# A vision-transformer layer on one core: PSUM slots of scores and mixes, and SBUF slots of the exps, taken strictly in turn

## The chip, the core and the metric

The kernel runs on one core of a Trainium2 chip. A core has five engines with instruction queues of their own: TensorE (PE), VectorE (DVE), ScalarE (ACT), GpSimd (POOL) and SyncE (SP, which here only issues transfers). They wait for each other through semaphores. The metric is the device time of one execution in microseconds; of the kernel before, six runs are at hand.

## The reference

The input is 16 images of 3x512x512. Each is cut into 1024 patches of 16x16, which become tokens of 256 values. One transformer layer follows. What matters here is its attention, eight heads of 32, in which the keys pass through a Fourier series of 256 frequencies before they are used:

```
q, k, v = to_heads(q), to_heads(k), to_heads(v)
k = kan_transform(k, kan_a, kan_b)      # sum over f of a_f*sin(f*k) + b_f*cos(f*k)
dots = einsum('bhqd,bhkd->bhqk', q, k) * scale
attn = softmax(dots, axis=-1)
out = einsum('bhqk,bhkd->bhqd', attn, v)
```

After that come the output projection, a second layernorm, a shared three-layer network, and four expert networks of which each token uses the two with the highest gates.

## The kernel before, in words

**Pairs and groups.** An image has four pairs of heads, and a pair two blocks of 512 queries, so there are 128 attention blocks. A block goes through the 1024 keys in eight chunks `kc` of 128. The Fourier series of an image's keys is worked off in 32 groups, 512 in all.

**A group** (lines 945 to 1083). Angles come from DRAM as whole numbers, spread over the partitions, into two "wave" tiles `w` (eight slots) and one `f`. POOL multiplies them by each partition's frequency (L1009), ACT takes the sines (L1019), TensorE mixes the two wave tiles into one PSUM tile `kan` of 128x1024 (L1039), DVE multiplies that by `f` (L1053), and TensorE adds up over partitions (L1072). `kan` is free when the product on DVE is done.

**A chunk of a block** (lines 1132 to 1199). TensorE computes the scores of a chunk into one PSUM tile `sT` of 128x1024 (L1137). ACT takes the exp (L1154). For an even chunk it writes it to an SBUF tile `es`, and the score's PSUM tile is free. For an odd chunk it writes it in place, into PSUM, and DVE then adds the even chunk's exp and writes the sum to an SBUF tile `both` (L1169); only then is the odd chunk's PSUM tile free. (The values `v` are stored so that the even chunk's exp and the pair's sum give the right weighted sum.) TensorE weighs the values with `es` or `both` (L1184), into one accumulator `av`. `es` and `both` are free when their weighing is done, `es` also needs the pair sum done.

**Slots.** `kan` and `sT`, 512 + 1024 = 1536 tiles, come from one PSUM pool `big` of two slots under one tag (lines 126, 1034, 1135). A tile fills two banks, so the slots are banks 0 and 1, and 2 and 3. `es` and `both`, 1024 tiles, come from the SBUF pool `esp` of five slots under one tag (lines 121, 1153, 1168). With one tag the framework picks the slot that a new tile takes. In the built program the slot taken from `big` is in 1485 of 1534 cases the one whose last reader was written down first; whoever writes to it waits for that reader.

**What sets the order.** All instructions are laid by a planner in the kernel itself. TensorE's order is a string written out by hand, `ORDER` (line 65): M is a mix, S a score, W a weighing, R an adding-up, and digits are steps of four chains that carry tokens, norms, projections and the feed-forward networks. Eleven of the sixteen images share one repeated piece of it. The other engines are filled in greedily by due times that the planner reckons with costs of its own (`others`, line 408). Where it lays a score or a mix it holds that the tile two before must be free (L443), and for an exp or a pair sum that the tile five before must be free (L1159). Each engine works through its queue in that order and stops at the first instruction whose semaphores are not there.

```
at = begin(PE, deps + (bigs[-2:-1] if user else []))   # L443: the tile two before
old = att * NT + kc - NES                               # L1160: the tile five before
```

Of the kernel before, what the change touches and what calls it, by code (L numbers as in the profile page):

```python
# [11 lines left out]
FP = mybir.dt.float32  # L12
# [3 lines left out]
PSUM = bass.MemoryType.PSUM  # L16
DRAM = bass.MemoryType.DRAM

P = 128
# [3 lines left out]
N = 1024  # L23
NT = N // P
# [24 lines left out]
NES = 5  # L49
# [41 lines left out]
def plain_path(ctx: ExitStack, tc: tile.TileContext, a: dict, out: bass.AP, verdict: bass.AP):  # L91
# [14 lines left out]
    def pool(name, bufs, space=None):  # L106
        kw = {} if space is None else {"space": space}
        return ctx.enter_context(tc.tile_pool(name=name, bufs=bufs, **kw))
# [9 lines left out]
    wp = pool("wp", NW)  # L118
    fp = pool("fp", GS)
    srcp = pool("srcp", 1)  # L120
    esp = pool("esp", NES)
    q4p = pool("q4p", 2)
    ffp = pool("ffp", 1)
    ff2 = pool("ff2", 2)
    smp = pool("smp", 1)
    big = pool("big", 2, PSUM)
    side = pool("side", 1, PSUM)
    redp = pool("redp", 1, PSUM)
    avp = pool("avp", 1, PSUM)
# [131 lines left out]
    def put(engine, queue, cost, deps, key, action):  # L261

        queues[engine].setdefault(queue, []).append((cost, deps, key, action))
# [29 lines left out]
    def side_tile(name):  # L293

        i = chains[now["chain"]]["bank"] = banks(now["chain"])[0][1]
        return side.tile([P, 512], FP, tag=f"side{i}", name=name)
# [729 lines left out]
    kan = {}  # L1026
    red = {}
    bigs = []

    def mix(g):  # L1030


        def action():
            ps = kan[g] = big.tile([P, N], FP, tag="big", name="kan")
            for j in range(2):
                w = w_tiles.pop((g, j))
                for blk in range(2):
                    for r in range(2):
                        nc.tensor.matmul(  # L1039
                            out=ps[ds(64 * j + 32 * blk, 32), ts(r, 512)],  # L1040
                            lhsT=coef[ts(r, 64)].rearrange("p e f j -> p (e f j)"),
                            rhs=w[ts(r, 64), ts(blk, 512)],
                            start=True,
                            stop=True,
                        )

        deps = [("sine", g, 0), ("sine late", g)]
        put(PE, "M", 0.86, deps, ("mix", g), action)
# [79 lines left out]
    scores = {}  # L1128
    exps = {}
    acc = {}  # L1130

    def score(att, kc):
        def action():
            q4 = bands_of_queries[att]
            ps = scores[kc] = big.tile([P, 1024], FP, tag="big", name="sT")
            for s in range(2):
                nc.tensor.matmul(  # L1137
                    out=ps[:, ts(s, 512)],
                    lhsT=k4[:, 2 * s + kc // 4, ts(kc % 4, P)],
                    rhs=q4[:, s, :],  # L1140
                    start=True,
                    stop=True,
                )

        deps = [("stacked", att // 2), ("q4", att)]
        put(PE, "S", 0.47, deps, ("score", att, kc), action)

    def exponential(att, kc):
        def action():
            now["table"] = AF.Exp  # L1150
            ps = es = scores[kc]
            if kc % 2 == 0:
                es = exps[kc] = esp.tile([P, 1024], FP, tag="es", name="es")
            nc.scalar.activation(es, ps, AF.Exp, scale=SCALE)  # L1154

        deps = [("score", att, kc)] + (tile_free(att, kc) if kc % 2 == 0 else [])
        put(ACT, "fixed", 0.99, deps, ("exp", att, kc), action)

    def tile_free(att, kc):  # L1159
        old = att * NT + kc - NES  # L1160
        if old < 0:
            return []
        deps = [("av", *divmod(old, NT))]
        return deps if old % 2 else [*deps, ("sum", *divmod(old + 1, NT))]

    def pair_sum(att, kc):
        def action():
            both = exps[kc] = esp.tile([P, 1024], FP, tag="es", name="both")
            nc.vector.tensor_add(both, scores[kc], exps[kc - 1])  # L1169

        deps = [("exp", att, kc - 1), ("exp", att, kc)] + tile_free(att, kc)
        put(DVE, "sum", 1.16, deps, ("sum", att, kc), action)
# [114 lines left out]
    for rd in range(B * RI + 2):  # L1287
        groups = range(GS * rd, min(GS * rd + GS, total))
        att = rd - 2
# [26 lines left out]
    ps = side_tile("okT")  # L1316
# [583 lines left out]
def vit_layer(tc: tile.TileContext, a: dict, out: bass.AP):  # L1900
    with tc.tile_pool(name="verdict", bufs=1) as vp:
        verdict = vp.tile([1, 1], mybir.dt.int32, tag="verdict", name="verdict")
        plain_path(tc, a, out, verdict)
        bad = tc.nc.values_load(verdict[0:1, 0:1], min_val=0, max_val=1)
        with tc.If(bad > 0):
            general_path(
                tc, *(ap for name, ap in a.items() if name not in PLAIN_ONLY), out
            )
# [149 lines left out]
```

## Time and profile before

| | |
|---|---|
| Median of six runs | 3968.06 us (3959.48 to 3974.56) |
| The profiled execution | 3971.46 us, span 3969.9 us |
| Mean granted TensorE clock | 0.984 |
| TensorE busy | 3726.7 us, 94% of the span |
| ScalarE busy | 3259.3 us, 82% |
| GpSimd busy | 3191.6 us, 80% |
| VectorE busy | 3116.9 us, 79% |
| Transfers | 915.93 MB, 231 GB/s on average |

The profile is one execution on the chip. Busy time says how long an engine worked, and the list of waits says what ended the idle time of an engine: "PE sT L1137 <- ACT es L1154: 51.0, 71, 3.2" means that TensorE stood idle before score matmuls until an exp had ended, 51.0 us in all, 71 times, 3.2 us at most. PEld is TensorE's loading of weights, which runs ahead of the matmuls and carries their waits; a wait there costs only what its matmul also waits. "Issue" is idle time for which no other instruction is found. A line of the order in time gives start, duration, engine, line, operation, tiles, and in brackets the idle time before it.

### The profile page before, as it was taken

What the parts mean: (1) busy time and instruction counts of PE and PEld (TensorE: products, weight loads), DVE (VectorE), ACT (ScalarE), POOL (GpSimd) and SP (SyncE); (2) the same over time, 40 slices, a digit from 0 to 9 for tenths busy, and PEclk for the clock granted to TensorE, in tenths of its full rate; (3) what the DMA queues carried; (4) which work ended last, traced back from release to release, by engine and by line L of the source; (5) the groups of instructions that cost most, each with busy time, mean ns of one, the idle gap of its engine ahead of it and who ended that gap; (6) DMA issues with size and microseconds to landing.
All of it is one profiled execution on the core that took longest, in us unless ns stands there. A gap on an engine that the chain in (4) does not pass through costs nothing. (4 is left out here: it accounts for less than half of the span.)

```text
span 3969.9 us, 93620 instructions
## 1 busy us (share of the span) xinstructions
PE 3726.7 (94%) x35701; PEld 1808.4 (46%) x35701; DVE 3116.9 (79%) x4715; ACT 3259.3 (82%) x3875; POOL 3191.6 (80%) x2312
## 2 busy tenths in 40 slices
PE   6888999999999999999999999999999999999988
PEld 4324344454444445454454444545444454534434
DVE  4777878878787888878878787887878878788873
ACT  2687888888888888888888888888888888888983
POOL 4988888788888878888888888878878888888860
PEclk9999999999999999999999999999999999999999
DMA  7887877888888788878888788888878888778750
GB/s 233 267 234 207 265 220 232 250 234 258 215 251 239 218 262 235 250 225 246 240 244 250 216 241 241 224 252 237 242 222 250 243 235 252 212 233 246 217 165 21
DMA packets 587580, 915.93 MB, mean 231 GB/s; under 512 B 58828, under 2 KB 177524, under 8 KB 587124
## 3 DMA queue, kind: packets, MB, share of 16 engines
q1 hardware_dynamic: 580880, 906.98, 78.4%
q8 instruction: 285, 4.67, 0.5%
q10 hardware_dynamic: 6244, 2.88, 0.3%
q14 instruction: 171, 1.40, 0.1%
HBM read 758.64 MB, written 150.99 MB: 229 GB/s over the span
## 5 line engine op out<-in xcount | busy, mean ns | idle before, releaser
L1009 POOL TENSOR_TENSOR w<-w,lane 128x1024 int32<-128x1024 int32 x1024 | 1924.7, 1895 | 388.7 <-DMA w<-ud 288.6
L1019 ACT ACTIVATE w<-w 128x1024 f32<-128x1024 int32 x1024 | 1011.6, 1047 | 52.4 <-POOL w L1009 48.7
L1009 POOL TENSOR_TENSOR f<-f,lane 128x1024 int32<-128x1024 int32 x512 | 970.1, 1895 | 103.6 <-DVE f L994 99.5
L1137 PE MATMUL sT<-q,k 128*128 128x512 f32 x2048 | 746.8, 464 | 163.7 <-DVE both L1169 55.2
L1169 DVE TENSOR_TENSOR both<-sT,es 128x1024 f32<-128x1024 f32 x512 | 624.3, 1219 | 308.7 <-ACT sT L1154 295.5
L1154 ACT ACTIVATE sT<-sT 128x1024 f32<-128x1024 f32 x512 | 517.4, 1011 | 266.9 <-PE sT L1137 197.4
L1053 DVE TENSOR_TENSOR f<-kan,f 128x1024 f32<-128x1024 f32 x512 | 609.1, 1214 | 144.8 <-ACT f L1019 91.3
L994 DVE STREAM_SHUFFLE f<-src 128x1024 int32<-128x1024 int32 x512 | 687.9, 1360 | 0.4
L1154 ACT ACTIVATE es<-sT 128x1024 f32<-128x1024 f32 x512 | 521.4, 1018 | 123.8 <-PE sT L1137 112.8
L1137 PEld LDWEIGHTS sT<-q,k 128*128 128x128 f32 x2048 | 344.8, 192 | 557.5 <-ACT es L1154 172.8
L1039 PE MATMUL kan<-w,coef 64*32 64x512 f32 x8192 | 556.4, 604 | 21.3 <-ACT w L1019 19.9
L1019 ACT ACTIVATE f<-f 128x1024 f32<-128x1024 int32 x512 | 517.3, 1047 | 0.0
L1184 PE MATMUL av<-both,v 128*32 128x256 f32 x4096 | 326.9, 390 | 4.1 <-DVE both L1169 3.8
L1184 PE MATMUL av<-es,v 128*32 128x256 f32 x4096 | 323.1, 386 | 3.6 <-DVE rc L1225 3.4
L1184 PE MATMUL av<-both,ones 128*32 128x256 f32 x4096 | 321.9, 385 | 0.0
L1072 PE MATMUL red<-f,pack 128*32 128x512 f32 x2048 | 301.8, 614 | 4.4 <-DVE f L1053 2.5
L1208 DVE RECIPROCAL rc<-av 128x256 f32<-128x256 f32 x128 | 224.4, 1753 | 66.1 <-PE av L1184 66.0
L1039 PEld LDWEIGHTS kan<-w,coef 64*32 64x32 f32 x8192 | 119.5, 106 | 303.4 <-issue 131.2
L301 PE MATMUL tok<-wt,x 128*128 128x256 f32 x960 | 226.4, 387 | 16.3 <-DMA w1s<-in_sW 13.1
L301 PEld LDWEIGHTS tok<-wt,x 128*128 128x128 f32 x960 | 181.3, 192 | 73.0 <-issue 20.4
L1184 PEld LDWEIGHTS av<-es,v 128*32 128x32 f32 x4096 | 110.5, 109 | 195.8 <-issue 153.7
L1184 PEld LDWEIGHTS av<-both,v 128*32 128x32 f32 x4096 | 115.0, 110 | 170.3 <-issue 95.6
(154 smaller groups left out, 4823.1 us busy)
## 6 DMA issues: line engine op xcount, KB each, us to landing
w<-ud SPq DMA_DIRECT2D x2048, 256.0 KB
q<-qd SPq DMA_DIRECT2D x512, 128.0 KB
k<-kd SPq DMA_DIRECT2D x128, 512.0 KB
x<-in_xT SPq DMA_DIRECT2D x128, 384.0 KB
ud<-u SPq DMA_DIRECT2D x64, 512.0 KB
ud<-ui SPq DMA_DIRECT2D x64, 512.0 KB
src<-ud SPq DMA_DIRECT2D x512, 64.0 KB
qd<-qhi SPq DMA_DIRECT2D x64, 256.0 KB
```

The costliest lines, as they stand in the source:

```text
L301: nc.tensor.matmul(out=out, lhsT=lhsT, rhs=rhs, start=start, stop=stop)
L994: nc.vector.stream_shuffle(w, sources[g // 8].rearrange("p r n -> p (r n)"), [4 * (g % 8) + i // 8 for i in range(32)],)
L1009: nc.gpsimd.tensor_tensor(w, w, f.to_broadcast([P, N]), ALU.mult)
L1019: nc.scalar.activation(x, w, AF.Sin, scale=TURN * 2.0**-32)
L1039: nc.tensor.matmul(out=ps[ds(64 * j + 32 * blk, 32), ts(r, 512)], lhsT=coef[ts(r, 64)].rearrange("p e f j -> p (e f j)"), rhs=w[ts(r, 64), ...
L1053: nc.vector.tensor_mul(w, kan.pop(g), w)
L1072: nc.tensor.matmul(out=rows_of_pair[p][ts(2 * i + r, 32), :], lhsT=pack[:, ds(PACK0 - 16 * (k % 2) - 2 * (k // 2), 32)], rhs=prod[:, ts(r, ...
L1137: nc.tensor.matmul(out=ps[:, ts(s, 512)], lhsT=k4[:, 2 * s + kc // 4, ts(kc % 4, P)], rhs=q4[:, s, :], start=True, stop=True,)
L1154: nc.scalar.activation(es, ps, AF.Exp, scale=SCALE)
L1169: nc.vector.tensor_add(both, scores[kc], exps[kc - 1])
L1184: nc.tensor.matmul(out=acc[0][ts(i, HD), ts(half, 256)], lhsT=ones32 if half else v[:, kc, p % NPAIR, ts(i % 2, HD)], rhs=es[:, ds(512 * ( ...
L1208: nc.vector.reciprocal(rc[0], acc[0][:, 256:512])
```

## The change

The two pools keep their slots, but each slot gets a tag of its own, and the kernel names the tag. For `big` the tag is the parity of the count of scores and mixes laid so far, so the two slots are taken strictly in turn. For `esp` it is the number of the chunk over all blocks, modulo five. The string of TensorE's order and the planner stay as they are.

```diff
-    esp = pool("esp", NES)
+    esp = pool("esp", 1)
...
-    big = pool("big", 2, PSUM)
+    big = pool("big", 1, PSUM)
...
-            ps = kan[g] = big.tile([P, N], FP, tag="big", name="kan")
+            ps = kan[g] = big.tile([P, N], FP, tag=f"big{len(bigs) % 2}", name="kan")
...
-            ps = scores[kc] = big.tile([P, 1024], FP, tag="big", name="sT")
+            ps = scores[kc] = big.tile([P, 1024], FP, tag=f"big{len(bigs) % 2}", name="sT")
...
-                es = exps[kc] = esp.tile([P, 1024], FP, tag="es", name="es")
+                es = exps[kc] = esp.tile([P, 1024], FP, tag=f"es{(att * NT + kc) % NES}", name="es")
...
-            both = exps[kc] = esp.tile([P, 1024], FP, tag="es", name="both")
+            both = exps[kc] = esp.tile([P, 1024], FP, tag=f"es{(att * NT + kc) % NES}", name="both")
```

## The prediction

> **What bounds the kernel now.** I read the page's first part, then the list of waits, then the groups by line, and last the order in time around single scores.
>
> The page shows TensorE at 94%, no other engine above 82%, a granted clock of nine tenths or more in every slice, and a chain of waits in which no line holds over 1.2%. So there is no single bottleneck to remove: TensorE works through one list written out by hand, and the time is its work plus the short stops in that list. Its idle time is 3969.9 - 3726.7 = 243 us, of which 160 - 118.4 = 42 us lie in the first 160 us (busy time by stretch).
>
> ```profile
> PE 3726.7 (94%) x35701; PEld 1808.4 (46%) x35701; DVE 3116.9 (79%) x4715; ACT 3259.3 (82%) x3875; POOL 3191.6 (80%) x2312
> PEclk9999999999999999999999999999999999999999
> ```
>
> The change decides which of two PSUM slots a score or a mix is written to, so what counts is TensorE's wait for a slot. In the list of waits (total us, times, longest) these rows are such waits, or their echo one engine further:
>
> ```profile
> DVE both L1169 <- ACT sT L1154: 295.5, 238, 3.6
> ACT sT L1154 <- PE sT L1137: 197.4, 171, 4.9
> PE sT L1137 <- DVE both L1169: 55.2, 58, 4.1
> PE sT L1137 <- ACT es L1154: 51.0, 71, 3.2
> PE sT L1137 <- DVE f L1053: 21.0, 35, 3.1
> ACT es L1154 <- PE av L1184: 8.3, 7, 2.5
> ```
>
> The reader is to see that TensorE stood still 127 us (55.2 + 51.0 + 21.0) before scores, half of its idle time, and that it waits about as long for a pair sum (DVE, L1169) as for an exp (ACT, L1154). A score of an even key chunk is read by its exp alone, so an exp frees its slot. A score of an odd chunk is read by its exp, which stays in PSUM, and then by the pair sum, which frees it. The groups by line give what each takes:
>
> ```profile
> L1169 DVE TENSOR_TENSOR both<-sT,es 128x1024 f32<-128x1024 f32 x512 | 624.3, 1219 | 308.7 <-ACT sT L1154 295.5
> L1154 ACT ACTIVATE es<-sT 128x1024 f32<-128x1024 f32 x512 | 521.4, 1018 | 123.8 <-PE sT L1137 112.8
> ```
>
> (The page's line for L1154 shows the same figures.)
>
> **The change, part by part.** The built programs have the same instructions in the same order on all five engines, DMA issues included; only slots and the waits that follow from them differ. SP's and POOL's waits are the same too. Nothing is moved past a queue.
>
> *The exps' five slots.* 442 of 1024 exps and pair sums get another slot. In the trace I compared the start of each of the 1024 writes with the end of the last reader of the slot that it will have: all find it free, the tightest by 0.065 us, nineteen in twenty by over 0.87 us. Price taken: 0. Bounds: at best the 8.3 us of the row above that ends in "PE av" is saved, at worst as much is added. The cover is that five slots are more than the list keeps in use. ScalarE gets 243 more semaphore instructions in front of its activations; in the trace sines with none ahead start 96 ns before the one before them ends, and sines with one start 94 ns before, so I take 243 x 0.002 = 0.5 us on an engine that is 82% busy: nothing.
>
> *The two PSUM slots.* 549 of 1536 scores and mixes change slot, all in pairs of neighbours: 275 times a tile took the slot of the tile just before it, and the next one took the other; with the change each takes the slot of the tile two before. In 249 of the 275 the first of the pair is an odd score which waited for the exp of the even score just before it, and will wait for the pair sum of the odd score before that one. Which comes first? With ScalarE back to back, the even exp starts about 0.09 us before the odd exp ends, and takes 1.02; the pair sum starts 0.03 after the odd exp and takes 1.22. So the pair sum frees its slot 0.03 + 1.22 - (1.02 - 0.09) = 0.32 us later. Over the 275 the new releaser ends later in 204, and the median difference is 0.32 us.
>
> A place where the change costs, in order of time (start, duration):
>
> ```profile
> 1908.55 1.01 ACT L1154 ACTIVATE sT<-sT 128x1024 f32<-128x1024 f32 x1
> 1909.47 1.02 ACT L1154 ACTIVATE es<-sT 128x1024 f32<-128x1024 f32 x1
> 1909.59 1.22 DVE L1169 TENSOR_TENSOR both<-sT,es 128x1024 f32<-128x1024 f32 x1 [1.30 <-ACT sT L1154]
> 1910.54 0.77 PEld L1137 LDWEIGHTS sT<-q,k 128*128 128x128 f32 x4
> ```
>
> The score's weights load at 1910.54, 0.05 after the exp's end (1910.49). The pair sum ends at 1910.81, so with the change they load at 1910.86: 0.32 us later, of which 0.25 shows on TensorE, because the matmul before it was still running.
>
> A place where it gains:
>
> ```profile
> 1883.13 1.23 DVE L1169 TENSOR_TENSOR both<-sT,es 128x1024 f32<-128x1024 f32 x1
> ...
> 1884.14 1.02 ACT L1154 ACTIVATE es<-sT 128x1024 f32<-128x1024 f32 x1 [0.38 <-PE sT L1137]
> 1885.21 0.30 PEld L1137 LDWEIGHTS sT<-q,k 128*128 128x128 f32 x2 [1.56 <-ACT es L1154]
> 1885.21 0.74 PE L1137 MATMUL sT<-q,k 128*128 128x512 f32 x2 [1.11 <-ACT es L1154]
> ```
>
> Here ScalarE had other work, so the exp came late and the pair sum was done at 1884.36: with the change the score starts at 1884.41 instead of 1885.21, 0.80 us earlier.
>
> Doing the same for all 275: in 116 TensorE starts the first tile later, by 43.4 us in all (0.37 each); in 31 earlier, by 13.1 us (0.42 each); in the other 128 the slot is free in either case. Raw sum +30.3 us.
>
> What is late next? Behind the score on TensorE stand the next score, then weighings (av) and mixes, which hardly wait (3.8 + 3.4 us and 21.3 us in the whole trace by the list of waits and the groups); they move with it until TensorE reaches a stop that it would have made anyway (a sine not yet done, keys or pair sum not there), and that stop swallows the rest. I followed each pair down the queues with the trace's own rows: same order, each row its measured duration, its start the later of the row before it and the end of what releases it plus the 0.05 us these rows show, transfers their measured time from issue to landing. The losses of 43.4 us have shrunk to 31.8 within 5 us, to 24.8 after 20 and to 21.7 by the end (82 pairs left). The gains keep 10.9 of 13.1 (27 pairs). Sum: 21.7 - 10.9 = +10.8 us; all 275 moved together give +11.0, most of it in the first 900 us and the last 450, with gains and losses nearly level between. Bounds: nothing swallowed, +30; all losses swallowed and all gains kept, -13. I take +11, because that is read from each place, and keep both ends.
>
> ScalarE's own gain is in this sum: in before 123 exps follow at once on the exp that freed their score's slot, which leaves ScalarE idle 0.88 us each time (at 1885.16 above), and with the change 4 do. But ScalarE's idle time costs only where TensorE later waits for it.
>
> A rule speaks against my sign. The Trainium skill, page "Perfetto Trace Analysis", section "Optimizing Tensor Performance", says that independent matmul groups should rotate through the PSUM banks, so that emptying one overlaps the next group's matmuls. The kernel before breaks that rotation 275 times and the changed one never; by the rule only the gains would count, about -13 us. The trace agrees at 1885.21 and disagrees at 1910.54, where the bank that the rotation names is the one emptied last.
>
> **The sum.** The profiled execution took 3971.46 us (span 3969.9), 3.4 above the median of the runs, 3968.06. 3971.5 + 11 + 0 + 0 = 3982.5; less 3.4, 3979 us, or +0.28%. A measurement of this kernel can tell about 0.2%, 8 us, from no change.
>
> **The rivals.**
>
> *Faster: the rotation wins.* The mechanism is the gain at 1885.21: the score no longer queues behind its neighbour's exp. It has 13.1 us raw and decides if of the losses' 43.4 us less than 5 survive, instead of 21.7; then the sum is below -8. For it: the 197.4 us that ScalarE's in-place exps wait for their scores are an effect of such neighbours. Against: 204 of 275 new releasers end later, and the pair sum is the longer chain by construction of the odd chunk. Price at most -13: 3955.
>
> *No measurable difference.* More of the losses vanish in stops of TensorE than I read, say 14 of 43.4 survive, and 11 gained: +3, 3971. For it: in the middle of the run gains and losses are already level, and 54 of the 82 surviving losses, 9.4 of the 21.7 us, are steps under 0.3 us. Against: the tally's losses stop shrinking after 50 us (21.3 by then).
>
> *Much slower.* The late scores make exps, pair sums and mixes late, mixes free the wave tiles late, and the loads behind them (POOL already waits 288.6 us for them) come late too: nothing is swallowed and something added, +30 or more, 3998. Against: the tally moves those loads too, and its sum falls over the first 50 us instead of growing.
>
> *The change does nothing to the waits* can be ruled out for PSUM, where 549 slots differ; for the exps it is what I forecast.
>
> **How the numbers follow.** Forecast case (+4 to +20) 0.62, no measurable difference beyond that 0.23, much slower 0.09, faster 0.06. About 0.09 of the forecast case lies under 8 us. So slower by over 0.2%: 0.62 - 0.09 + 0.09 = 0.62; within: 0.23 + 0.09 = 0.32; faster: 0.06. The range runs from -4 (half of the no-difference case and the faster one left out) to +26 (near the bound at which nothing is swallowed): 3964 to 3994.
>
> **What would show it.** In the waits after, TensorE's scores waiting for pair sums should rise from 55.2 us to about 95, and those waiting for exps (ACT es) fall from 51.0 to about 20; together up by some 10. ScalarE's wait of in-place exps for scores should stay near 200 us or rise by up to 20, and no row of exps waiting for weighings should grow. TensorE's busy time should be the same within a few us, with the added time all idle. The prediction is wrong if the waits for exps go without the waits for pair sums rising, if transfers or the clock differ, or if the added time sits at another line than the scores'.

## The result, and the profile after

The changed kernel took 3975.07 us (median of 29 runs), the kernel before, measured beside it, 3968.6 us (66 runs). The ratio is 1.0018, with an interval of 1.0012 to 1.0023: slower by 7.1 us, 5 to 9. The forecast was +11 us and lay on the right side; by the bound of 0.2% stated with it, the measured +0.18% is just inside "no difference".

The first lines of the changed kernel's page:

```profile
span 3977.0 us, 93841 instructions
PE 3731.6 (94%) x35701; PEld 1807.1 (45%) x35701; DVE 3118.5 (78%) x4715; ACT 3258.0 (82%) x3875; POOL 3192.0 (80%) x2312
PEclk9889999999999999999999999999999999999999
```

The work is the same on every engine. TensorE's busy time is 4.9 us longer than before at a mean granted clock of 0.982 instead of 0.984. That belongs to this one execution: in a second profiled execution of the changed kernel, with the clock at 0.984, TensorE was busy for 3725.1 us, less than the 3726.7 before.

The list of waits of the changed kernel (total us, times, longest), and last the row for the stacked keys in the kernel before:

```profile
DVE both L1169 <- ACT sT L1154: 305.8, 247, 3.5
ACT sT L1154 <- PE sT L1137: 247.8, 229, 4.9
PE sT L1137 <- DVE both L1169: 91.8, 138, 3.8
PE sT L1137 <- DMA k<-kd: 30.2, 19, 3.3
PE sT L1137 <- ACT es L1154: 19.5, 30, 3.2
PE sT L1137 <- DVE f L1053: 16.3, 35, 3.4
...
PE sT L1137 <- DMA k<-kd: 19.4, 11, 3.3
```

The reader is to see the exchange. Scores waited 55.2 us for pair sums and 51.0 us for exps; now it is 91.8 and 19.5. That the three rows for slots add up to 127.6 us, as before (127.2), does not mean that the exchange was free: each row carries several us of one execution's chance. In the second profiled execution of the changed kernel the same rows add up to 131.6 us, and the wait for the transfer of the stacked keys, 10.8 us above before here, is 21.8 us and only 2.4 above. The steadier figure is the idle time before all score matmuls together, in the groups by line, before and after:

```profile
L1137 PE MATMUL sT<-q,k 128*128 128x512 f32 x2048 | 746.8, 464 | 163.7 <-DVE both L1169 55.2 <-ACT es L1154 51.0 <-DVE f L1053 21.0
...
L1137 PE MATMUL sT<-q,k 128*128 128x512 f32 x2048 | 746.3, 464 | 168.9 <-DVE both L1169 91.8 <-DMA k<-kd 30.2 <-ACT es L1154 19.5
```

That is +5.2 us, and +4.5 in the second execution. All idle time of TensorE together (span less busy time) rose less, from 243.2 to 245.4 us, in both executions by about 2. The experiments below are compared by the idle time before scores too.

The costly place of the prediction, the same score, in the order of time of the changed kernel:

```profile
1913.64 1.01 ACT L1154 ACTIVATE sT<-sT 128x1024 f32<-128x1024 f32 x1
...
1914.56 1.02 ACT L1154 ACTIVATE es<-sT 128x1024 f32<-128x1024 f32 x1
...
1914.68 1.23 DVE L1169 TENSOR_TENSOR both<-sT,es 128x1024 f32<-128x1024 f32 x1 [1.20 <-ACT sT L1154]
1915.96 0.76 PEld L1137 LDWEIGHTS sT<-q,k 128*128 128x128 f32 x4 [0.34 <-DVE both L1169]
```

The even exp ends at 1915.58, the pair sum at 1915.91, and the score's weights load at 1915.96, 0.05 after the pair sum and 0.38 after the exp that released it before. Both exps come 5.09 us later than in the trace of before and the weights 5.42: the place costs 0.33 us, where the prediction said 0.32.

The gaining place of the prediction:

```profile
1889.15 1.22 DVE L1169 TENSOR_TENSOR both<-sT,es 128x1024 f32<-128x1024 f32 x1
...
1889.43 0.74 PE L1137 MATMUL sT<-q,k 128*128 128x512 f32 x2
1890.27 1.02 ACT L1154 ACTIVATE es<-sT 128x1024 f32<-128x1024 f32 x1 [0.44 <-PE sT L1137]
...
1890.43 0.73 PE L1137 MATMUL sT<-q,k 128*128 128x512 f32 x2 [0.26 <-DVE both L1169]
```

The score starts 0.06 us after the pair sum and no longer waits for the exp, which has only begun: 1.00 us behind the score before it, where it was 1.85.

### The profile page after: what moved, and what is told of

The parts are those of the page before. It is cut to its first block, busy times and chain, and to the rows that moved or that the text cites. A ratio compares the mean times of both kernels' runs of the same rounds, so it can differ in the third digit from the quotient of the medians.

```text
span 3977.0 us, 93841 instructions
## 1 busy us (share of the span) xinstructions
PE 3731.6 (94%) x35701; PEld 1807.1 (45%) x35701; DVE 3118.5 (78%) x4715; ACT 3258.0 (82%) x3875; POOL 3192.0 (80%) x2312
## 4 chain that ended last, share of the span: by engine, by line
PE 45%; ACT 13%; DMA 10%; DVE 10%; POOL 6%; issue 4%; SPq 1%; ACTq 0%; POOLq 0%; DVEq 0%
PE av L1184 10%; PE sT L1137 8%; DMA w<-ud 5%; PE kan L1039 5%; ACT w L1019 5%; DVE both L1169 4%; POOL w L1009 4%; PE red L1072 3%; PE e1p L301 3%; ACT sT L1154 3%; ACT f L1019 2%; PE tok L301 2%; PE q L301 2%; DMA k<-kd 2%; PE tok L304 1%
## 5 line engine op out<-in xcount | busy, mean ns | idle before, releaser
L1137 PE MATMUL sT<-q,k 128*128 128x512 f32 x2048 | 746.3, 464 | 168.9 <-DVE both L1169 91.8
L1154 ACT ACTIVATE sT<-sT 128x1024 f32<-128x1024 f32 x512 | 517.6, 1011 | 270.9 <-PE sT L1137 247.8
L301 PE MATMUL tok<-wt,x 128*128 128x256 f32 x960 | 226.0, 387 | 15.8 <-DMA x<-in_xT 12.7
```

What stands on the lines that cost most here:

```text
L301: nc.tensor.matmul(out=out, lhsT=lhsT, rhs=rhs, start=start, stop=stop)
L1137: nc.tensor.matmul(out=ps[:, ts(s, 512)], lhsT=k4[:, 2 * s + kc // 4, ts(kc % 4, P)], rhs=q4[:, s, :], start=True, stop=True,)
```

## The experiments

In these kernels the PSUM slots are given by a list of places. Tiles are counted in the order in which TensorE writes them. A tile takes the slot of the tile two before, as in the changed kernel, unless its number is in the list `NEWER`; then it takes the slot of the tile just before it. The list of all 275 places makes the slots of the kernel before, the empty list those of the changed kernel. "Costly", "gaining" and "other" places are the 116, 31 and 128 of the prediction, read from the trace of before alone. Unless something else is said, the exps keep their one tag with five slots. Differences in us are the ratio less one, times the median of the kernel before in the same comparison. The lists are long: where a diff only changes the list, a comment stands for it.

My theory: the two PSUM slots alone matter, place by place, by which of two releasers ends later; part of the delays is swallowed, that is, made up for at a later stop that TensorE makes anyway. Rivals: the exps' slots, or the 243 more semaphore instructions that stand on ScalarE, cost something; the cost is spread and not in the places; a score that starts earlier only runs into the next stop.

### The parts of the change

**Only the PSUM pool in turn.** The diff to the kernel before:

```diff
-    big = pool("big", 2, PSUM)
+    big = pool("big", 1, PSUM)
...
-            ps = kan[g] = big.tile([P, N], FP, tag="big", name="kan")
+            ps = kan[g] = big.tile([P, N], FP, tag=f"big{len(bigs) % 2}", name="kan")
...
-            ps = scores[kc] = big.tile([P, 1024], FP, tag="big", name="sT")
+            ps = scores[kc] = big.tile([P, 1024], FP, tag=f"big{len(bigs) % 2}", name="sT")
```

> Only the PSUM pool's slots are taken in turn; the exps keep one tag with five slots, as before. Theory (the slot of an odd score is freed by the later of two releasers): all of the change's cost is here, +5 to +11 us on the kernel before (it was +7.1, ratio 1.0018), and TensorE's score waits for pair sums near 92 us. Rival (the exps' slots, or the 243 semaphore instructions that they put on ScalarE, make up part of the cost): clearly less than the whole change, under +4 us.

Measured: ratio 1.0010 (1.0001 to 1.0019), +4.0 us, 0.4 to 7.6. Scores waited 95.7 us for pair sums, and idle time before scores was 174.0 us. The waits moved as in the whole change. The time alone could not tell this from the rival; the next run does, as far as the exps' slots go.

**Only the exps' slots in turn**, with all 275 places in `NEWER`, so that PSUM is as before (the code that reads the list is shown under "Costly places alone"):

```diff
-    esp = pool("esp", NES)
+    esp = pool("esp", 1)
...
-                es = exps[kc] = esp.tile([P, 1024], FP, tag="es", name="es")
+                es = exps[kc] = esp.tile([P, 1024], FP, tag=f"es{(att * NT + kc) % NES}", name="es")
...
-            both = exps[kc] = esp.tile([P, 1024], FP, tag="es", name="both")
+            both = exps[kc] = esp.tile([P, 1024], FP, tag=f"es{(att * NT + kc) % NES}", name="both")
```

> Only the exps' slots are taken in turn; every score and mix is given, by a list of places, the PSUM slot that it had before. Theory: 0 us, within 2, no wait row moves by more than 5 us. Rival (exps' slots or ScalarE's semaphore instructions cost): +3 us or more, with exps or pair sums waiting for weighings.

Measured: ratio 0.9997 (0.9986 to 1.0009), -1.2 us, -5.6 to +3.6; scores waited 53.8 us for pair sums and 53.0 for exps, idle time before scores 162.6 us. The exps' slots cost nothing that can be measured, and that rival falls. The semaphore instructions are not tested by this run: counted in the built programs, ScalarE has 1605 of them here, 1622 in the kernel before and 1865 in the changed one, and 1795 with only the PSUM pool in turn. So it is the PSUM slots that bring most of them. No run isolates them. What speaks against a cost of theirs are two runs below, the costly and the other places alone: they have 1682 and 1680, and differ by 18 us.

**Only the exps' slots in turn, PSUM left to the framework.** The same diff, without a list.

> The exps' slots in turn, the PSUM pool left with one tag, so that the framework picks its slots again. In the built program it then picks otherwise in 29 places, nearly all of them gaining ones. Theory (places decide): -9.1 us by the trace, -5 to -13, although the exps' slots by themselves are worth nothing. Rival (exps' slots are all that differs): 0, as in the run that held the PSUM slots.

Measured: ratio 0.9970 (0.9959 to 0.9981), -11.9 us, -16 to -8. One half of the change, taken alone, makes the kernel faster, and by something that its diff does not name: in the built program the framework's pool hands out the PSUM slots differently in 29 places once the exps are not its business any more; 23 of them are gaining ones and 2 costly. The list of waits shows the same exchange as the change, but smaller, with the exps now losing more than the pair sums gain:

```profile
PE sT L1137 <- DVE both L1169: 64.4, 79, 3.1
PE sT L1137 <- ACT es L1154: 39.0, 56, 3.2
```

Waits for pair sums rose by 9 us (55.2 to 64.4) and those for exps fell by 12 (51.0 to 39.0). The idle time before scores does not show the gain: it is 167.4 us in this profile, 3.7 above before. The profiled execution took 3974.94 us and was the slowest of the twelve, so its trace can't show the gain as a whole.

### The places

**Costly places alone.** The list is the 275 without the 116 costly ones.

```diff
+NEWER = {
+    19, 44, 63, ...
+}
...
+    turn = [1, 0]
+
+    def slot():
+        if len(bigs) - 1 not in NEWER:
+            turn.reverse()
+        return turn[0]
...
-            ps = scores[kc] = big.tile([P, 1024], FP, tag="big", name="sT")
+            ps = scores[kc] = big.tile([P, 1024], FP, tag=f"big{slot()}", name="sT")
```

> The PSUM slots are swapped in only those 116 of the 275 places in which the trace of before said that the pair sum ends later and TensorE has to wait for it; everywhere else the slots are those of before. Theory: +21.9 us (read from the trace: 43.4 raw, half swallowed), 15 to 27. Rival (the places' losses are swallowed and the cost of the change is spread over all): not over +9.

Measured: ratio 1.0038 (1.0024 to 1.0052), +15.1 us, 10 to 21. Twice the cost of the whole change, as the theory says and the rival does not. It is less than the +21.9 forecast, which lies just outside the interval. The groups by line show 181.9 us of idle time before scores, 18.2 more than before:

```profile
L1156 PE MATMUL sT<-q,k 128*128 128x512 f32 x2048 | 745.4, 463 | 181.9 <-DVE both L1188 83.6 <-ACT es L1173 43.8 <-DMA k<-kd 21.0
```

**Gaining places alone.** The same kernel with the 275 without the 31 gaining ones in the list.

```diff
-NEWER = {   # 275 places without the 116 costly
+NEWER = {   # 275 places without the 31 gaining
```

> The PSUM slots are swapped in only the 31 places in which the trace of before said that TensorE waits for the neighbour's exp although the pair sum is done. Theory: -10.6 us (13.1 raw, most of it kept), -6 to -13, faster than both kernels. Rival (a score that starts earlier only runs into the next stop): 0, within 3.

Measured: ratio 0.9972 (0.9959 to 0.9986), -11.1 us, -16 to -6; faster than both kernels and at the forecast -10.6. The rival falls: what a score gains by starting earlier is kept.

```profile
L1161 PE MATMUL sT<-q,k 128*128 128x512 f32 x2048 | 749.3, 465 | 153.6 <-DVE both L1193 60.7 <-ACT es L1178 33.5 <-DMA k<-kd 22.6
```

Idle time before scores is 153.6 us, 10.1 less than before: the gain in time is this idle time.

**The other places alone.** The 275 without the 128 others.

```diff
-NEWER = {   # 275 places without the 31 gaining
+NEWER = {   # 275 places without the 128 others
```

> The PSUM slots are swapped in the 128 places in which the trace of before has the slot free either way. Theory: 0.0 us, within 3. Rival (part of the cost sits where no wait was seen): +3 or more, and with the costly and the gaining places the three runs then don't add up to the whole change.

Measured: ratio 0.9993 (0.9980 to 1.0006), -2.8 us, -8 to +2: nothing that can be measured. Nearly half of the swaps are free. The three kinds of places together make +15.1 - 11.1 - 2.8 = +1.2 us, with an uncertainty of some 9 us: no contradiction to the whole change, but no proof that it is the sum either.

**The best choice that I found.** Gaining places as above, and three places more that the other way round get the slot of the tile just before; the list then has 247 numbers.

```diff
+    99,
...
+    120,
...
+    1505,
```

> As the run with the gaining places, with three more places swapped that the trace of before says to be worth 0.08 us or more each. Theory: -12.4 us on the kernel before, -7 to -16; no other choice of the two slots that I found in the trace gives more, so this is about what the choice of slots can bring. Rival: as before, 0.

Measured: ratio 0.9957 (0.9942 to 0.9971), -17.1 us, -23 to -12. This kernel beats both without an instruction of work less. Whether the three more places did anything over the -11.1 of the gaining ones can't be told: the intervals overlap. Idle time before scores, 154.1 us, speaks against it, and so does the comparison at equal clock further down.

### Where the losses went

All costly places together cost a third less than forecast. Three runs split them, and a fourth repeats the change on the same chip. All four were compared with the kernel before there.

**The costly places in the middle.** The list is the 275 without the 75 costly places between 900 and 3500 us of the trace of before:

```diff
-NEWER = {   # 275 places without the 116 costly
+NEWER = {   # 275 places without the 75 costly in the middle
```

> Of the 116 costly places only the 75 between 900 and 3500 us are swapped, raw 25.3 us. Theory as I sized it: +11.1 us. Rival for the shortfall of the run with all costly places (+15 measured, +21.9 forecast): in the middle, where transfers and other stops are densest, more is swallowed than one execution's trace says: 0 to +6.

Measured: ratio 1.0004 (0.9992 to 1.0016), +1.6 us, -3 to +6. The forecast, +11.1, is out. But idle time before scores rose by 8.6 us:

```profile
L1158 PE MATMUL sT<-q,k 128*128 128x512 f32 x2048 | 744.3, 462 | 172.3 <-DVE both L1190 66.8 <-ACT es L1175 55.3 <-DVE f L1074 18.1
```

**The costly places at the two ends.**

```diff
-NEWER = {   # 275 places without the 75 costly in the middle
+NEWER = {   # 275 places without the other 41 costly
```

> The other 41 costly places, before 900 and after 3500 us, raw 18.1 us. Theory as I sized it: +10.9 us. If the shortfall is in the middle, this one keeps its +9 to +12; if losses are over-sized everywhere by a third, +7.

Measured: ratio 1.0029 (1.0013 to 1.0045), +11.5 us, 5 to 18, at the forecast of +10.9. Idle time before scores rose by 7.1 us, less than with the middle alone:

```profile
L1160 PE MATMUL sT<-q,k 128*128 128x512 f32 x2048 | 745.4, 463 | 170.8 <-DVE both L1192 73.9 <-ACT es L1177 42.3 <-DMA k<-kd 21.4
```

**The swallowed places.** These are costly places whose delay, followed through the trace of before, is gone later.

```diff
-NEWER = {   # 275 places without the other 41 costly
+NEWER = {   # 275 places without the 34 whose delay is swallowed
```

> The 34 costly places whose delay the trace says is swallowed by a stop that TensorE makes anyway, raw 10.4 us of later starts. Theory: +0.6 us, within 3. Rival (a late score costs what it is late): +10 us.

Measured: ratio 1.0001 (0.9988 to 1.0015), +0.4 us, -5 to +6. Delays that the trace said are swallowed are; the rival's +10 is out.

**The change again**, without an edit.

> The changed kernel itself once more, on the chip of the three runs beside it, so that the places can be summed against it. Theory: +7 us (ratio 1.0018), between +5 and +9; costly places and gaining places together then make the change: about +15 and -11 by the earlier runs, +4, or +21.9 and -10.6, +11, by the forecast.

Measured: ratio 1.0014 (1.0000 to 1.0028), +5.6 us, 0 to 11: no contradiction to the first result. Middle and ends, +1.6 and +11.5, make 13.1 of the 15.1.

By these medians the losses in the middle vanish and those at the ends are as forecast. That is not shown, because the granted clock differs between the executions. Its mean over the twelve was 0.9838 for the middle and 0.9824 for the ends, and 0.9832 for the kernel before. Within one and the same kernel, an execution whose clock is 0.001 higher is 3.2 us shorter (a fit over the 207 executions of these runs and of the kernel before beside them, with a mean for each kernel). The table gives what is left at equal clock, an estimate from this fit that takes the clock for chance of the executions and not for an effect of the slots; it is uncertain by about 2.5 us, and by 3.3 for the two runs with six executions (costly places, best choice).

| us against the kernel before | by the ratio | at equal clock | idle before scores |
|---|---|---|---|
| the change again | +5.6 | +2.5 | +4.5 |
| PSUM pool alone | +4.0 | +2.7 | +10.3 |
| exps alone, PSUM as before | -1.2 | 0.0 | -1.1 |
| exps alone, PSUM left to the framework | -11.9 | -7.6 | +3.7 |
| costly places | +15.1 | +13.1 | +18.2 |
| gaining places | -11.1 | -11.2 | -10.1 |
| other places | -2.8 | -2.4 | -2.3 |
| best choice | -17.1 | -10.7 | -9.6 |
| costly, middle | +1.6 | +5.7 | +8.6 |
| costly, ends | +11.5 | +7.3 | +7.1 |
| costly, swallowed | +0.4 | +0.1 | -1.6 |

At equal clock middle and ends cost about the same, 5.7 and 7.3 us, and make up the 13.1 of all costly places. Both stay below their forecasts, 11.1 and 10.9. So the term that was too large is the surviving losses as a whole, and not those of the middle alone. The gains are at their forecast. Of the whole change the repeat leaves +2.5 us, 0 to 5; for the first comparison the clocks of the kernel before are not on record, so how much of its 7.1 us is clock can't be said.

Where the missing losses went stays open. I laid the traces side by side, TensorE instruction by instruction. In the run with the middle places alone, the first matmuls of the 75 tiles fall back by 24.7 us in all against the matmul before them (forecast 25.3), and 10 us further on the delay is still 26.7 (forecast 18.4). After 20 us it is -0.1, where 12.6 was forecast. But that last sum is not to be trusted: in two runs that swap nothing in the middle it is -2.8 (exps alone, PSUM as before) and -10.9 (ends), so the comparison with one execution of before brings in a chance of several us. One source of such chance is the transfer of the stacked keys, for which scores wait 16 to 31 us in all in the runs of the table. I had moved each transfer with its own measured time from issue to landing. For these 128 transfers that time is 6.3 us on average, but one and the same transfer differs from the execution of before by a standard deviation of 0.4 to 0.6 us in every run where it was compared: more than the mean loss of a costly place, which is 0.4 us. That such waits swallow the delays is a guess that no run here tests.

### Taking the cause away

If the odd score's longer chain is the cause, freeing its slot by the exp, as for the even score, should remove it. This is the changed kernel with the odd exp written straight to the SBUF tile of the pair's sum, to which the pair sum then adds. All five engines keep their order.

```diff
-            if kc % 2 == 0:
-                es = exps[kc] = esp.tile([P, 1024], FP, tag=f"es{(att * NT + kc) % NES}", name="es")
+            name = "both" if kc % 2 else "es"
+            es = exps[kc] = esp.tile([P, 1024], FP, tag=f"es{(att * NT + kc) % NES}", name=name)
             nc.scalar.activation(es, ps, AF.Exp, scale=SCALE)
...
-            both = exps[kc] = esp.tile([P, 1024], FP, tag=f"es{(att * NT + kc) % NES}", name="both")
-            nc.vector.tensor_add(both, scores[kc], exps[kc - 1])
+            nc.vector.tensor_add(exps[kc], exps[kc], exps[kc - 1])
```

> The changed kernel, but the exp of an odd chunk is written to the SBUF tile of the pair's sum and the pair sum adds to it there, so that the exp frees the odd score's PSUM slot too, and the order of all engines stays. It takes the supposed cause away: the slot in turn is then never the one freed last. Theory: TensorE's score waits for pair sums (91.8 us) go to 0, those for exps rise, and by the trace's rows moved accordingly the time falls by 45 us on the changed kernel and 35 on the one before, 25 to 40, as long as the pair sum takes 1.22 us with both inputs in SBUF and POOL's products 1.90. Rival (two engines on SBUF get in each other's way): pair sums or POOL's rows L1009 are longer, 1536 x 0.1 us = 150 us on an engine busy 80%, and the time rises by 10 us or more. Rival (the waits for pair sums are only a place where TensorE's idle time shows): within 8 us of the changed kernel.

Measured: 4212.16 us, ratio 1.0610 (1.0594 to 1.0627), +242 us. The first rival holds, by far more than it was priced at. The waits of scores for pair sums are gone, as the cause's removal asks: the list of waits has none, and idle time before scores falls to 149.5 us from 168.9. But the groups by line say what it was bought with; the first row is that of the kernel before:

```profile
L1009 POOL TENSOR_TENSOR w<-w,lane 128x1024 int32<-128x1024 int32 x1024 | 1924.7, 1895 | 388.7 <-DMA w<-ud 288.6 <-PE sT L1137 19.8 <-ACT hT L524 18.8
...
L1009 POOL TENSOR_TENSOR w<-w,lane 128x1024 int32<-128x1024 int32 x1024 | 2142.6, 2106 | 221.5 <-DMA w<-ud 174.3 <-ACT f L1019 8.1 <-PE sT L1137 7.0
L1009 POOL TENSOR_TENSOR f<-f,lane 128x1024 int32<-128x1024 int32 x512 | 1099.6, 2148 | 77.1 <-DVE f L994 70.7 <-DMA qd<-qhi 2.4 <-DMA w<-ud 2.0
L1168 DVE TENSOR_TENSOR both<-both,es 128x1024 f32<-128x1024 f32 x512 | 985.8, 1926 | 219.8 <-ACT both L1154 215.9
```

A pair sum takes 1926 ns on average instead of 1219, a product on POOL 2106 and 2148 instead of 1895. The order in time shows how:

```profile
2124.45 1.89 POOL L1009 TENSOR_TENSOR f<-f,lane 128x1024 int32<-128x1024 int32 x1
2124.76 2.66 DVE L1168 TENSOR_TENSOR both<-both,es 128x1024 f32<-128x1024 f32 x1 [2.03 <-ACT both L1154]
2126.30 4.72 POOL L1009 TENSOR_TENSOR w<-w,lane 128x1024 int32<-128x1024 int32 x2
```

The pair sum starts while POOL multiplies (until 2126.34), and ends 1.08 us after that: it did its work only then. Of the 375 pair sums that start inside a product, nine in ten end 1.08 to 1.16 us after it. POOL's next two products, from 2126.30, take 0.94 us longer than two otherwise do. So this run can't say what the shorter chain would be worth, and the size of the cause is shown by the places alone.

## Why the prediction was right, and where it was off

*The exps' slots: 0.* Right: -1.2 us, -5.6 to +3.6. The 243 more semaphore instructions do not belong to this term, as I had put it: the exps' slots alone bring none, the PSUM slots most (1795 against 1622), and no run isolates their cost. What I did not see either is that the exps' tags change the slots that the framework picks in the other pool (29 places, -11.9 us by themselves). In the whole change this has no part, since both pools are in turn there.

*Which releaser is later.* Right in sign, and nearly in size: against the matmul before them, the first matmuls of the costly places at the two ends start later by 14.2 us in the changed kernel's trace (18.1 forecast), those in the middle by 21.3 (25.3), and those of the gaining places earlier by 13.4 (13.1). So some 8 us of the 43.4 us of losses are not there to begin with; in the run with the costly places alone it is 5.

*Gains kept: 10.9 of 13.1.* Right: -11.1 us alone, -11.2 at equal clock, where -10.6 was forecast for these places.

*Losses that survive: 21.7 of 43.4.* This is the term that was mis-sized. The losses measure +15.1 us, 10 to 21, and 13.1 at equal clock; by the latter figure the places in the middle and those at the ends both fall short. The forecast's +11 became +7.1, and in the repeat +5.6, or +2.5 at equal clock. That the first result came as near to +11 as it did may be partly luck with the clock.

*The rule on rotation.* The Trainium skill's sentence (page "Perfetto Trace Analysis", section "Optimizing Tensor Performance"), taken literally, puts only gains on this change. The places measure both sides: where the rotation's slot is the one emptied first, keeping it is worth 11 us, and where it is the one emptied last, it costs 15 (13 at equal clock).

*What the waits would show.* Pair sums to about 95 us (91.8 and, in the repeat, 90.7), exps to about 20 (19.5 and 19.9): right. That they would together be up by some 10 us was not so: it is 5.1 and 4.4 in the two executions, and idle time before scores rose by 5.2 and 4.5. That the added time would be all idle can't be read from them either: TensorE's whole idle time rose by about 2 us in both. ScalarE's wait of in-place exps for scores rose to 247.8 us and not by at most 20; but all idle time before these exps rose only from 266.9 to 270.9:

```profile
L1154 ACT ACTIVATE sT<-sT 128x1024 f32<-128x1024 f32 x512 | 517.4, 1011 | 266.9 <-PE sT L1137 197.4 <-issue 46.4 <-ACT es L1154 15.8
...
L1154 ACT ACTIVATE sT<-sT 128x1024 f32<-128x1024 f32 x512 | 517.6, 1011 | 270.9 <-PE sT L1137 247.8
```

In the kernel before, 46.4 us of it stood under "issue" and 15.8 under the exp before it. Most of the rise is the wait under another name.

*The rivals.* "Faster" needed fewer than 5 us of surviving losses and had 13 to 15. "Much slower" did not come: fewer losses survive than forecast, not more. "No measurable difference" supposed that 14 us of losses survive and 11 are gained, +3 in all, and by the places it is the nearest: 15.1 and 11.1, or 13.1 and 11.2 at equal clock. The first comparison's time, +7.1, lies midway between it and the forecast, and the repeat can't part them.

## What to carry to other kernels

With two slots whose users are freed after chains of different length, "strictly in turn" is not the same as "the one that is free first"; a planner that assumes the one and a framework that does the other differ in both directions, and the net of about +13 to +15 and -11 us looks like a small matter. Read from the trace, place by place, which releaser ends later and whether the queue stands there; then choose each slot by hand: here that brought about 0.3% with the same work. Before a difference of this size is put down to one part of a change, compare the granted clocks of the executions: here they made two halves of the losses look like 2 and 12 us that are nearer to 6 and 7. And before a buffer is moved from PSUM to SBUF to shorten such a chain, look at what VectorE and POOL read from SBUF at that time.

## What the runs showed of the hardware that I had not expected

An addition on VectorE with both inputs in SBUF and POOL's products take turns. In the run with the odd exp in SBUF, 26 pair sums met no work of POOL and took 1224 ns (median), as they do with one input in PSUM; 385 that lay wholly beside POOL's work took 2107 ns. Products of POOL that met no pair sum took 1892 ns (894 of 1536). Of the 368 that started inside a pair sum the median is 2872 ns; of the 1168 others, whether a pair sum joined them or not, all but one kept their 1.9 us. With the odd exp in PSUM, in the kernel before, pair sums beside POOL's products take 1224 ns and the products 1895. The Trainium skill says on its page "SBUF — State Buffer", section "Who interferes with whom", that a VectorE instruction with two inputs in SBUF contends with a GpSimd instruction that reads SBUF. These runs agree and give the price: about one microsecond to whichever comes second, here 375 pair sums and 368 products. The time rose by 242 us with it. Part of that may be the granted clock, 0.976 to 0.978 in this run against 0.984 before: by the 3.2 us for 0.001 found above, some 20 to 25 us, an estimate.
